# The border before the mixing: weights of group 32 in the forward stage, special columns with the others, the last spectrum store in two parts

## The chip, the cores and the metric

The kernel runs on one core of one Trainium2 chip. The metric is the device time of one execution in microseconds (us), as the median of several runs. Beside it there is one execution that the hardware profiler recorded; all durations of single instructions are taken from that one.

## The reference

The input x is `(16, 16, 256, 256)` in float32: 16 images, 16 channels, 256 rows, 256 columns. Two layers are computed, each of the form x + f(group norm of x).

```python
# layer 0: 3x3 circular convolution, written in the frequency domain
Kx = jnp.fft.ifft2(x, norm='ortho')
z = jnp.einsum('oihw,bihw->bohw', Lw, Kx)
y = jnp.real(jnp.fft.fft2(z, norm='ortho'))
...
# layer 1: Laplace operator with poles and residues
alpha = jnp.fft.fft2(x, axes=(-2, -1))
A = 1.0 / (omega1[:, None, None, None] - weights_pole1[None])
Bm = 1.0 / (omega2[:, None, None, None] - weights_pole2[None])
S = jnp.einsum('ikpq,oikp,xikq->oxik', weights_residue, A, Bm)
output_residue1 = jnp.einsum('biox,oxik->bkox', alpha, S)
output_residue2 = jnp.einsum('bikpq,ikpq->bkpq', D, weights_residue)
x1 = jnp.fft.ifft2(output_residue1, axes=(-2, -1)).real
x2 = jnp.einsum('kbiqz,biqx->kizx', F, E2).real
return x1 + x2 / Nx / Ny
```

S mixes the 16 input channels into 16 output channels with a matrix of its own for every frequency. That product is the mixing stage below; the two-dimensional transform before it is the forward stage.

## The kernel before

There are four stages after one another, which share one SBUF and one set of queues.

1. The convolution with its norm (`conv`, up to line 713), some 565 us. Its result v goes to DRAM in `vD`.
2. The forward transform (lines 716 to 980), until about 1197 us. Its loop goes over 64 units: channel i, outer, and four images at a time. In each unit `fold` makes even and odd parts, `lines` transforms one direction on TensorE, and `columns` the other; the first result is copied to SBUF as `q` (L833) and combined on VectorE into the spectrum tile `spec` (L837 to L840). `first_slots` sets a few special columns (L848 on VectorE, L849 on GpSimd), and after the four units of a channel `project` multiplies (`pr`, L865, VectorE) and adds (`proj`, L866, GpSimd), and `spec` is stored to `aD` in DRAM (L976). The spectrum tile alternates between two pools, `spec_even` and `spec_odd`; the last channel uses `spec_odd`. The last store goes through ScalarE's queue, the others through SP's.
3. The mixing (lines 984 to 1248), until about 1860 us: 32 groups of frequencies. A row of `aD` for a partition is one frequency of the other direction; group g takes partitions 4g to 4g+3. For each group a tile of mixing matrices `sg` is made: `weights(g)` computes small pole terms on VectorE (L903 to L919) and spreads them into `w` (L930 on GpSimd; for group 0 four copies on ScalarE, L927); `sums` multiplies `w` with the constant table `ct` on TensorE (L1032), and `spread` puts the result into `sg`, one half by ScalarE (L1049), one by a shuffle on VectorE (L1052). `mix` is the product with the loaded spectrum `abd` (L1120), its result goes through `yt` (L1233) to `yD` in DRAM (L1134). While group g is mixed in four quarters n, the sums of group g+1 are made, one quarter ahead of each mixing.
4. The inverse transform (lines 1251 to 1451).

The border that matters here is `first_sums` (L1054): the matrices of group 0. That group holds two special frequencies, so the halves of its `sg` come from two sets of weights, those of group 0 and those of an extra group 32. `first_sums` clears `abd01` (L1058), computes the weights of 0 (begun in the forward stage) and of 32, loads the first spectrum quarters (`load`, L1102), adds `accs` (L1062), goes through two halves h of four quarters n with sums and spreads, and fixes one column of each half with a copy of the other set's column, kept in `other` (L1078, L1079). Between the quarters it computes the weights of group 1. At the end it clears `abd2` and `abd3` (L1081) and loads them (L1107). `finish_projections` then forms `o2` from `accs` and the constant `jmat` (L1090 to L1092), and the loop over groups begins.

Three things set the order. Instructions run on each engine's queue in the order in which the program emits them, except that the framework moves what is emitted outside the stages with a written order (`manual_schedule`) to where its inputs are free. Pools of different stages lie over each other in SBUF: a tile of the mixing may be written when the tile of the forward stage that lay there has been released by its last reader, a store included. `abd3` and the second `sg` pool (`sg1`) lie over `spec_odd`. And a DMA's issue waits in SP's queue behind the one before it[...].

Of the kernel before, what the change touches and what calls it, by code (L numbers as in the profile page):

```python
# [16 lines left out]
B = 16  # L17
# [7 lines left out]
def conv_then_laplace_kernel(ctx: ExitStack, tc: tile.TileContext, a: dict, out: bass.AP):  # L25
# [36 lines left out]
    o2 = cp.tile([P, B, 2, 16], FP, name="o2", tag="o2")  # L62
    proj = cp.tile([P, 2, B, 16, 2], FP, name="proj", tag="proj")
    jmat = cp.tile([P, 3, P], FP, name="jmat", tag="jmat")
# [93 lines left out]
    nc.sync.dma_start(out=jmat, in_=a["jmat"])  # L158
# [573 lines left out]
    u0 = pool(p1, "u0")  # L732
# [140 lines left out]
    up = {"v": pool(p2, "v", side="right"), "u0": u0}  # L873
# [21 lines left out]
    def weights(g):  # L895
# [4 lines left out]
        u = up["u" if g else "u0"].tile([P, 4, 32, 4], FP, name="u", tag="u")  # L900
# [19 lines left out]
        if g == 0:  # L920
            yield
# [3 lines left out]
        if g == 0:  # L925
            for i in range(4):
                nc.scalar.activation(w4[:, :, i], v2, AF.Copy, scale=m4[:, i : i + 1])  # L927
            return wt
# [14 lines left out]
    last, first_weights = None, weights(0)  # L943
    for u in range(len(units) + 1):
# [23 lines left out]
        if u == len(units) - 4:  # L968
            first_constants()
        if len(units) - 4 < u < len(units):  # L970
            next(first_weights)
        if last is not None:
            first_slots(b0, spec, *done)
            if b0 == B - 4:
                project(i, psd)
                (nc.sync if i + 1 < C else nc.scalar).dma_start(  # L976
                    out=aD[:, 2 * i : 2 * i + 2], in_=spec.rearrange("p r f b -> p r (f b)")
# [20 lines left out]
    def new_sg(g):  # L998
        return (g0, g1)[g % 2].tile([P, N, 2 * C], FP, name="sg", tag="sg")
# [8 lines left out]
    zp.tile([P, 384], FP, name="between", tag="between")  # L1008
# [16 lines left out]
    def sums(n, w):  # L1025

        ps = [pg.tile([P, 2, N], FP, name="ps_s", tag="ps_s") for _ in range(2)]
        for q in range(2):
            for iq in range(4):
                for odd in range(2):  # L1030
                    rows = slice(64 * odd, 64 * odd + 64)
                    nc.tensor.matmul(  # L1032
                        ps[odd][32 * iq : 32 * iq + 32, q],
                        lhsT=w[rows, iq, 2 * n + q],
                        rhs=ct[rows, iq, 2 * n + q],
# [18 lines left out]
    def first_sums():  # L1054
# [4 lines left out]
        wt, w128 = at_once(first_weights), at_once(weights(32))  # L1059
        load(0, 1)  # L1060
        steps, w1 = weights(1), None
        nc.vector.tensor_tensor(accs, proj[:, :, :, :, 0], proj[:, :, :, :, 1], ALU.add)  # L1062
        sg = new_sg(0)
        other = up["u"].tile([P, 2, 2 * C], FP, name="other", tag="other")
        for h, w in enumerate((wt, w128)):
            for n in range(4):
                fy = slice(P * h, P * h + P)
                ps = sums(n, w)
                spread(
                    n,  # L1070
                    (sg[:, fy], [z[:, :, fy].rearrange("p q n -> p n q") for z in ps]),
                    (other[:, 1 - h], [z[:, :, P * (1 - h)] for z in ps]),
                )
                if 4 * h + n in (3, 4, 5):
                    w1 = next_step(steps, w1)
# [534 lines left out]
```

## Time and profile before

| | |
|---|---|
| median of 3 runs | 2617.32 us |
| lowest and highest | 2607.34 and 2626.05 us |
| the profiled execution's own time | 2623.94 us |
| its span, first to last instruction | 2622.1 us |
| mean granted TensorE clock | 0.986 |
| TensorE (PE) busy | 2468.6 us |
| VectorE (DVE) busy | 1980.8 us |
| moved by DMA | 653.17 MB |

The page of the profile gives busy times by engine, then the span in 40 slices of 65.6 us, then the DMA queues, then the chain of work that ended last, and then the costliest groups of instructions. The timeline shows single instructions by their start; an idle time in brackets names what ended it. ACTq and SPq rows are DMA issues in the queues of ScalarE and SP. "PEld" is TensorE's load of weights, which runs beside its matmuls.

### The profile page before, as it was taken

To read this page: it belongs to the slowest core of one execution; us is meant where nothing else is said; L and a number is where in the kernel's file an instruction comes from. 1 tells how busy PE (TensorE), PEld (TensorE's weight loads), DVE (VectorE), ACT (ScalarE), POOL (GpSimd) and SP (SyncE) were. 2 spreads that over 40 slices of the span, in tenths; PEclk is the share of its full clock that TensorE was granted. 3 is DMA by queue.
4 is the path that set the end of the run, shared out by engine and by line. 5 is a ranking of instruction groups with operands and counts; after the bars stand their busy time and mean duration, and the time that the engine had idled before them with its cause. 6 is when DMAs were issued, how large, how long until landed. Compare 5 with 4: busy or idle time off the path is not lost.

```text
span 2622.1 us, 84262 instructions
## 1 busy us (share of the span) xinstructions
PE 2468.6 (94%) x35314; PEld 1885.3 (72%) x35314; DVE 1980.8 (76%) x3772; ACT 1432.6 (55%) x2599; POOL 1290.5 (49%) x1179
## 2 busy tenths in 40 slices
PE   5998999989999999998999999999799999999998
PEld 2444455567777777775878778788688888888887
DVE  7777788848888888887877878887276676667666
ACT  2565566666666666665666656666244444444443
POOL 1333378433333333333666645766555565555553
PEclk9999999989999999999999999999899999999999
DMA  7888878854655655655777777777988888888884
GB/s 274 276 279 282 294 270 294 297 211 177 240 195 209 242 220 194 245 225 190 225 229 214 226 225 222 222 227 228 253 302 289 291 292 279 299 289 287 291 287 174
DMA packets 318011, 653.17 MB, mean 249 GB/s; under 512 B 49174, under 2 KB 163990, under 8 KB 305728
## 3 DMA queue, kind: packets, MB, share of 16 engines
q1 hardware_dynamic: 316464, 640.57, 72.4%
q8 instruction: 278, 4.55, 0.7%
q0 software_dynamic: 896, 3.02, 0.4%
q10 hardware_dynamic: 272, 4.19, 0.4%
q14 instruction: 101, 0.83, 0.1%
HBM read 368.15 MB, written 280.36 MB: 247 GB/s over the span
## 4 chain that ended last, share of the span: by engine, by line
PE 58%; DVE 7%; DMA 4%; SPq 3%; ACT 3%; POOL 2%; issue 1%; ACTq 0%; DVEq 0%; POOLq 0%
PE ps_mix L1120 9%; PE ps_y L777 9%; PE ps_y L785 8%; PE ps_p L1361 7%; PE ps_f L1385 7%; PE ps_f L1386 7%; PE ps_x L820 5%; DMA yD<-yt 4%; PE ps_s L1032 2%; SPq L1134 2%; PE ps_h L1345 2%; PE psd L805 1%; DVE r L1394 1%; DVE ol L1396 1%; DVE ol L1397 1%
## 5 line engine op out<-in xcount | busy, mean ns | idle before, releaser
L1120 PE MATMUL ps_mix<-abd,sg 128*64 128x128 f32 x8192 | 482.2, 276 | 39.4 <-DMA yD<-yt 16.6
L1120 PEld LDWEIGHTS ps_mix<-abd,sg 128*64 128x64 f32 x8192 | 451.9, 138 | 92.9 <-ACT yt L1233 55.7
L1325 POOL TENSOR_TENSOR u<-yk 128x512 f32<-128x512 f32 (+1 forms) x268 | 358.2, 1369 | 314.7 <-PE ps_p L1361 249.1
L305 PE MATMUL ps_conv<-xt,wc 32*32 32x512 f32 x12288 | 445.6, 602 | 36.0 <-issue 26.1
L305 PEld LDWEIGHTS ps_conv<-xt,wc 32*32 32x32 f32 x12288 | 251.1, 103 | 217.6 <-issue 127.0
L793 ACT ACTIVATE t<-ps_y,vmr 128x384 f32<-128x384 f32 x512 | 297.1, 580 | 161.1 <-PE ps_y L785 161.1
L1052 DVE STREAM_SHUFFLE sg<-ps_s 128x512 f32<-128x512 f32 (+1 forms) x264 | 329.1, 1316 | 0.0
L777 PE MATMUL ps_y<-tabE,vq 128*128 128x256 f32 x1024 | 313.2, 388 | 11.0 <-DVE vq L766 9.4
L785 PE MATMUL ps_y<-tabO,vq 128*128 128x256 f32 x1024 | 305.9, 380 | 0.0
L275 POOL TENSOR_TENSOR pair<-pair,far 128x1024 f32<-128x1024 f32 x64 | 151.7, 2370 | 304.1 <-DVE pair L272 207.7
L1385 PE MATMUL ps_f<-pt,inv 128*128 128x256 f32 x1008 | 300.4, 380 | 0.0
L1386 PE MATMUL ps_f<-hs,ey 128*128 128x256 f32 x1008 | 299.8, 379 | 0.0
L1361 PEld LDWEIGHTS ps_p<-inv,u 128*128 128x128 f32 x2048 | 268.9, 193 | 35.4 <-POOL u L1329 10.9
L1389 DVE TENSOR_TENSOR r<-ps_f,q 128x256 f32<-128x256 f32 x256 | 107.0, 418 | 241.9 <-ACT q L1388 241.9
L1361 PE MATMUL ps_p<-inv,u 128*128 128x128 f32 x2048 | 276.2, 278 | 9.8 <-POOL u L1329 9.7
L1049 ACT ACTIVATE sg<-ps_s,mcol 128x512 f32<-128x512 f32 (+1 forms) x264 | 179.3, 689 | 192.2 <-DVE sg L1052 117.1
L777 PEld LDWEIGHTS ps_y<-tabE,vq 128*128 128x128 f32 x1024 | 189.6, 191 | 87.5 <-ACT q L833 51.2
L1388 ACT COPY q<-ps_f 128x256 f32<-128x256 f32 x256 | 95.4, 373 | 274.7 <-PE ps_f L1386 250.4
L1363 ACT COPY pt<-ps_p 128x512 f32<-128x512 f32 x256 | 151.5, 592 | 134.9 <-PE ps_p L1361 134.9
L765 POOL TENSOR_TENSOR vq<-vf 128x512 f32<-128x512 f32 x64 | 81.4, 1272 | 291.6 <-DVE vf L769 281.5
L785 PEld LDWEIGHTS ps_y<-tabO,vq 128*128 128x128 f32 x1024 | 195.4, 191 | 26.9
L1233 ACT COPY yt<-ps_mix 128x512 f32<-128x512 f32 x352 | 184.1, 592 | 55.8 <-DMA yD<-yt 42.2
(237 smaller groups left out, 3993.6 us busy)
## 6 DMA issues: line engine op xcount, KB each, us to landing
xt<-in_x SPq DMA_DIRECT2D x288, 258.0 KB
vD<-pair SPq DMA_DIRECT2D x256, 256.0 KB
yD<-yt SPq DMA_DIRECT2D x512, 128.0 KB
vl<-vD SPq DMA_DIRECT2D x128, 512.0 KB
out_y<-ol SPq DMA_DIRECT2D x128, 512.0 KB
s<-vD SPq DMA_DIRECT2D x126, 512.0 KB
aD<-spec SPq DMA_DIRECT2D x15, 4096.0 KB
yk<-yD SPq DMA_DIRECT2D x60, 1024.0 KB
```

What stands on the lines that cost most here:

```text
L305: nc.tensor.matmul(acc[r][32 * c : 32 * c + 32], lhsT=ready[b][0][rows, phase, tap], rhs=halves[b][u // 2][rows, q : q + 5 : 4, 2 - tap : ...
L777: nc.tensor.matmul(ps[:, 0:N], lhsT=vf[:, xo, 0, j], rhs=tabE[:, 0 : i + 2 : i + 1], start=True, stop=False, skip_group_check=True,)
L785: nc.tensor.matmul(ps[:, P : P + N], lhsT=vf[:, xo, 1, j], rhs=tabO[:, i : C + 1 : C - i], start=False, stop=True, skip_group_check=True,)
L793: nc.scalar.activation(t[:, xo, j].rearrange("p l n -> p (l n)"), ps[:, 0:384], AF.Copy, scale=vmr[:, 0, b0 + j, i : i + 1],)
L1049: nc.scalar.activation(to[..., k : k + 2], src[odd], AF.Copy, scale=nsgn)
L1052: nc.vector.stream_shuffle(to[..., C + k : C + k + 2], src[1 - odd], swap)
L1120: nc.tensor.matmul(ps[64 * t : 64 * t + 64, j], lhsT=sg[:, f : f + 2].rearrange("p f m -> p (f m)"), rhs=abd[jq][:, :, 2 * t + cc, 2 * jj ...
L1233: (nc.vector.tensor_copy if m >= (2 if late else 3) else nc.scalar.copy)(o, src)
L1325: nc.gpsimd.tensor_tensor(u[:, :, j].rearrange("p b (c n) -> p c b n", c=8), in0, in1, o)
L1361: nc.tensor.matmul(ps[:, at], lhsT=u[:, n], rhs=tab, start=True, stop=True)
L1385: nc.tensor.matmul(ps[:, e], lhsT=tab, rhs=pt[:, e], start=True, stop=False)
L1386: nc.tensor.matmul(ps[:, e], lhsT=ey[:, e], rhs=hs, start=False, stop=True)
```

## The change

- The weights of group 32 are computed in the forward stage, as those of group 0: the steps of both are spread over the last six units (before: those of group 0 over the last three), and both are spread into `w` by ScalarE.
- In `sums` the weights of group 32 are multiplied with the halves of `ct` in turned order, so that the 128 columns that are needed and the first column of the other half lie side by side. `sg` of group 0 has one column more (257), each spread takes 129 columns, and `other` is copied from `sg` by one ScalarE copy for each half.
- The weights of group 1 are computed in the loop, ahead of the first mixing; group 0 then makes no sums in its first quarter, one set in the second and in the third, and two in the fourth.
- The last spectrum store is cut: partitions 0 to 15, all that the first four groups read, go first through ScalarE's queue; partitions 16 to 127 go through SP's queue, behind the issue of the first load.
- `accs` is added on GpSimd. `jmat` is loaded at the border into the memory of `s_ex`, and `o2` takes the memory of `proj`; the room under "between" becomes 320 columns, and `u0` and `v` get two buffers.

```diff
-    o2 = cp.tile([P, B, 2, 16], FP, name="o2", tag="o2")
-    jmat = cp.tile([P, 3, P], FP, name="jmat", tag="jmat")
...
-    nc.sync.dma_start(out=jmat, in_=a["jmat"])
...
-    u0 = pool(p1, "u0")
+    u0 = pool(p1, "u0", 2)
...
-    up = {"v": pool(p2, "v", side="right"), "u0": u0}
+    up = {"v": pool(p2, "v", 2, side="right"), "u0": u0}
...
-        u = up["u" if g else "u0"].tile([P, 4, 32, 4], FP, name="u", tag="u")
+        u = up["u" if g % 32 else "u0"].tile([P, 4, 32, 4], FP, name="u", tag="u")
...
-        if g == 0:
+        if g % 32 == 0:
...
-    last, first_weights = None, weights(0)
+    last, first_weights = None, [weights(0), weights(32)]
...
-        if u == len(units) - 4:
+        if u == len(units) - 7:
             first_constants()
-        if len(units) - 4 < u < len(units):
-            next(first_weights)
+        if len(units) - 7 < u < len(units):
+            next(first_weights[(u - len(units)) // 3 + 2])
         if last is not None:
             first_slots(b0, spec, *done)
             if b0 == B - 4:
                 project(i, psd)
+                rows = slice(0, P if i + 1 < C else 16)
                 (nc.sync if i + 1 < C else nc.scalar).dma_start(
-                    out=aD[:, 2 * i : 2 * i + 2], in_=spec.rearrange("p r f b -> p r (f b)")
+                    out=aD[rows, 2 * i : 2 * i + 2],
+                    in_=spec[rows].rearrange("p r f b -> p r (f b)"),
                 )
...
-        return (g0, g1)[g % 2].tile([P, N, 2 * C], FP, name="sg", tag="sg")
+        return (g0, g1)[g % 2].tile([P, N + 1 - g % 2, 2 * C], FP, name="sg", tag="sg")[:, 0 : N + (g == 0)]
...
-    zp.tile([P, 384], FP, name="between", tag="between")
+    zp.tile([P, 320], FP, name="between", tag="between")
...
-    def sums(n, w):
+    def sums(n, w, turned=False):
...
+                    c = ct[rows, iq, 2 * n + q].rearrange("p (h n) -> p h n", h=2)
                     nc.tensor.matmul(
-                        ps[odd][32 * iq : 32 * iq + 32, q],
+                        ps[odd][32 * iq : 32 * iq + 32, q].rearrange("p (h n) -> p h n", h=2),
                         lhsT=w[rows, iq, 2 * n + q],
-                        rhs=ct[rows, iq, 2 * n + q],
+                        rhs=c[:, ::-1] if turned else c,
...
-        wt, w128 = at_once(first_weights), at_once(weights(32))
+        wt, w128 = (at_once(steps) for steps in first_weights)
         load(0, 1)
-        steps, w1 = weights(1), None
-        nc.vector.tensor_tensor(accs, proj[:, :, :, :, 0], proj[:, :, :, :, 1], ALU.add)
+        nc.sync.dma_start(
+            out=aD[16:P, 2 * C - 2 : 2 * C], in_=spec[16:P].rearrange("p r f b -> p r (f b)")
+        )
+        nc.gpsimd.tensor_tensor(accs, proj[:, :, :, :, 0], proj[:, :, :, :, 1], ALU.add)
...
-                fy = slice(P * h, P * h + P)
-                ps = sums(n, w)
+                ps = sums(n, w, h == 1)
+                fy = slice(P * h, P * h + P + 1)
                 spread(
-                    n,
-                    (sg[:, fy], [z[:, :, fy].rearrange("p q n -> p n q") for z in ps]),
-                    (other[:, 1 - h], [z[:, :, P * (1 - h)] for z in ps]),
+                    n, (sg[:, fy], [z[:, :, 0 : P + 1].rearrange("p q n -> p n q") for z in ps])
                 )
-                if 4 * h + n in (3, 4, 5):
-                    w1 = next_step(steps, w1)
+            nc.scalar.copy(other[:, 1 - h], sg[:, P * (1 + h)])
...
+    jmat = ep.tile([P, 3, P], FP, name="jmat", tag="s_ex")
+    nc.sync.dma_start(out=jmat, in_=a["jmat"])
...
+        o2 = cp.tile([P, B, 2, 16], FP, name="o2", tag="proj")
...
-    ahead, wt = first_sums()
-    finish_projections()
+    ahead, wt = first_sums(), None
+    o2 = finish_projections()
...
-            evict = sums(n, w_now) if ahead is not None else []
+            if g == 0 and n == 0:
+                w_now = at_once(weights(1))
+            sets = () if ahead is None else (n,) if g else ((), (0,), (1,), (2, 3))[n]
+            evict = [(j, sums(j, w_now)) for j in sets]
             yt = yp.tile([P, 2, 4 * B, 16], FP, name="yt", tag="yt")
-            if evict:
-                spread(n, (ahead, [z.rearrange("p q n -> p n q") for z in evict]))
+            for j, ps in evict:
+                spread(j, (ahead, [z.rearrange("p q n -> p n q") for z in ps]))
```

More of the change, by code (lines that the diff above doesn't have):

```diff
@@ L924, in weights @@
         w4 = wt.rearrange("p a k (i m) -> p (a k) i m", i=4)
-        if g == 0:
+        if g % 32 == 0:
             for i in range(4):
@@ L1082, in first_sums @@
             load(0, jq)
-        return sg, w1
+        return sg
+    jmat = ep.tile([P, 3, P], FP, name="jmat", tag="s_ex")
+    nc.sync.dma_start(out=jmat, in_=a["jmat"])
     def finish_projections():
+        o2 = cp.tile([P, B, 2, 16], FP, name="o2", tag="proj")
         for ro in range(2):
@@ L1092, in finish_projections @@
             nc.vector.tensor_copy(o2[:, :, ro], ps)
+        return o2
     def load(g, jq, rows=range(4)):
```

## The prediction

> **What bounds the kernel now.** I read the page from the top: busy times, slices, then the chain.
>
> ```profile
> span 2622.1 us, 84262 instructions
> PE 2468.6 (94%) x35314; PEld 1885.3 (72%) x35314; DVE 1980.8 (76%) x3772; ACT 1432.6 (55%) x2599; POOL 1290.5 (49%) x1179
> PE   5998999989999999998999999999799999999998
> PE 58%; DVE 7%; DMA 4%; SPq 3%; ACT 3%; POOL 2%; issue 1%; ACTq 0%; DVEq 0%; POOLq 0%
> ```
>
> TensorE (PE) is busy nearly everywhere and leads the chain. The whole edit acts in one gap: the border between the forward stage and the mixing, near 1200 us. So the timeline of the window 1180 to 1260 us is the view that decides. Columns: start, length, engine, line, what, and in brackets the idle time before with its releaser.
>
> ```profile
> 1190.19 6.93 POOL L1058 MEMSET abd<- 128x8192 f32 x1 [0.31 <-POOL spec L849]
> 1190.99 1.69 ACT L927 ACTIVATE w<-v,mcol 128x256 f32<-128x256 f32 x4
> 1196.91 1.28 DVE L865 TENSOR_TENSOR pr<-psd,coef 128x512 f32<-128x512 f32 x2
> 1197.46 0.39 ACTq L976 DMA_DIRECT2D aD<-spec  x1
> 1198.11 0.98 DVE L903 TENSOR_TENSOR u<-kgrp,pims 128x128 f32<-128x128 f32 x1
> ...
> 1203.03 0.72 DVE L1052 STREAM_SHUFFLE sg<-ps_s 128x256 f32<-128x256 f32 x1
> ...
> 1204.59 6.72 PE L1032 MATMUL ps_s<-ct,w 64*32 64x256 f32 x128 [9.01 <-ACT other L1049]
> ...
> 1209.20 2.57 SPq L1102 DMA_DIRECT2D abd<-aD  x4
> ...
> 1215.35 1.89 POOL L930 TENSOR_TENSOR w<-v,mcol 128x1024 f32<-128x1024 f32 x1 [10.50 <-DVE v L919]
> ...
> 1217.18 6.97 POOL L1081 MEMSET abd<- 128x4096 f32 x2
> ...
> 1219.12 4.00 PE L1120 MATMUL ps_mix<-abd,sg 128*64 128x128 f32 x64
> ```
>
> VectorE (DVE) leads: weights of group 32 from 1198.11 to 1202.4, `accs` until 1203.0, then 32 shuffles with the weights of group 1 between them, until the first mixing starts at 1219.12. Then TensorE goes at a beat of 4.67 us per quarter group (1.02 of sums, 3.65 of mixing, in the chain), with the second, third and fourth mixing at 1224.07, 1228.74 and 1233.41, and the first of group 1 at 1239.19. That last start is my yardstick: the mixing behind it is TensorE at its beat, so a shift there reaches the end.
>
> The table by stretches shows the last store and the clock (columns: us, busy of PE, PEld, DVE, ACT, POOL with counts, clock, DMA share, GB/s):
>
> ```profile
> 1196.00:1198.00 2.00, 0.00 (x0) 0.00 (x0) 2.00 (x7) 0.00 (x0) 1.76 (x4) 1.00 0.00 0
> 1204.00:1206.00 2.00, 1.41 (x32) 0.68 (x32) 2.00 (x11) 1.68 (x6) 0.85 (x1) 0.50 1.00 426
> 1208.00:1210.00 2.00, 1.88 (x40) 1.11 (x32) 1.84 (x11) 1.47 (x6) 0.00 (x0) 0.50 0.03 8
> ```
>
> The 4.19 MB store moves data from 1198 to 1208 (the DMA view of 1195 to 1240 gives its queue 22.0% of 45 us, 9.9 us), and TensorE, idle from 1195.6 to 1204.6, comes back at clock 0.50 until about 1210.
>
> [...]
>
> **The change, part by part.**
>
> (a) Weights of 32. Eight DVE instructions leave the border: 1198.11 to 1202.42, 4.3 us. In the forward stage they add about 2.7 us of DVE work (0.28+0.29+0.29+0.94+0.25+0.34+0.28+0.28) over six units of 9.6 us, in which TensorE sets the pace and DVE waits 1.96 to 4.71 us per unit for ScalarE (ACT): nothing, and without that cover 2.7 us. The product moves from POOL (2.21 us) to four more ACT instructions. The built order puts six of the eight copies ahead of the first q copy and two ahead of the second. Six at 0.42 from 1190.99 end at 1193.55; before, the q copy began at 1192.95. The chain q, spec, pr is 0.6 us later: +0.6, and pr ends at 1198.8.
>
> (b) accs to POOL: -0.6 us of DVE; on POOL some 1.4 us (nearest row: 1.37 for 128x512) behind proj, done near 1202.3, needed only by `ps_o`.
>
> (c) Special columns. 16 DVE shuffles of 2 elements go (each pushes the next by about 0.17), 16 of ACT too; two ACT copies and a wait each way come, some 0.4 us each: -2.0 us. [...]
>
> (d) Weights of 1 leave the shuffles: DVE ran them at 1209.7 to 1215.1 in the border for 3.1 us. They now run after the first mixing's inputs, while that mixing runs. -3.1 us.
>
> (e) So shuffles start at 1198.8. A quarter costs about 1.25 us warm (2 x 0.55 of DVE, plus a TensorE round of 1.02 through four PSUM buffers), 1.95 at half clock as at 1204.6 to 1206.6. Eight quarters, some cold: 10 to 12 us, plus 1.2 for the fix. First mixing at 1210.4 to 1212, 7 to 9 us before 1219.12. It has no sums of group 1 in front of it. It ends near 1215.
>
> (f) The store in two. Small: issued at 1198.05. Around its data the old store took 1.84 us (1197.46 to 1209.20 less 9.9). Data: 1.24 us if the rate holds (9.9/8)[...]. I take 3.0 as middle: landed at 1202.9 (1201.1 to 1204.9). SP then issues the four loads (2.57), and the large store at 1205.5. The loads took until about 1215.0 after an issue at 1209.2, 5.8 us, so they land at 1208.7, in time for (e). Behind them the large store: 9.9 x 112/128 = 8.7, to 1217.4, plus 1.2 of receipt as before: 1218.6. jmat waits for the last line transform only and is in SBUF near 1193: nothing.
>
> (g) What is late next. abd3 lies in the memory of the last spectrum tile. In before its memset waits for the one store, over by 1209, and the product w of group 1 (POOL L930) runs ahead of both memsets. In the built order of the changed kernel the memset of abd3 waits for both stores, and the product for group 1 stands behind it on POOL. TensorE's queue has the sums with those weights between the first and the second mixing. So: large store 1218.6, memset 3.52, product 1.89, sums at 1224.2. TensorE, idle from 1215, comes back cold: mixing costs 475 instead of 273 ns there, so 43% of about 4.7 us, 2.0 us. Second mixing ends at 1224.2+1.02+3.65+2.0 = 1230.9; third +4.67 = 1235.6; fourth with two sums +2.04+3.65 = 1241.3; sums 1.02: first mixing of group 1 at 1242.3. Before: 1239.19.
>
> (h) Three small loads of SP move from 497.6 to the first 50 us, jmat leaves there: both in queues TensorE does not wait for; 0, and 1 us either way without that.
>
> Sum at the yardstick: -4.3-0.6-2.0-3.1+0.6 = -9.4 at the first mixing (-7 to -9 by timeline with the cold rounds), then all of it lost at the new wait: +3.1. On the profiled execution's 2623.94 us (span 2622.1) that is 2627.0; that execution is 6.6 us over the median of the runs, 2617.32, so for the median 2620.4.
>
> **Rivals.**
> B, the wait does not bind. Were the product ahead of the abd3 memset in effect, or the store done by 1210, group 1's weights would be there and the border keep its 7 to 9 us: 2609.5. For it: only DMA times stand between. Against: the store would need to move 3.67 MB in under 2 us. A partial form is likelier: small store at full rate and a warm clock give 1224.2-1.8-2.0, a yardstick of 1238.5, -0.7: 2616.6.
> C, slower: [...] +7.1, 2624.4. [...] Against: the stretch 1228 to 1230, with yD stores of 32 partitions each in it, carries 268 GB/s.
> D, much slower: the 112-partition store runs on few engines. One engine of 16 moves 4.19 MB/16 in 9.9 us; on four engines 3.67 MB take 35 us, 26 more: from there on the change is slower by over 1%, 2647; on one 139 us, 2750. [...]
> That the change does not do what it says: the built order shows every part in place.
>
> **How the numbers follow.** A (the wait takes the gain, +1 to +5) 0.53; C 0.17; B in its partial form 0.15, full 0.08; D 0.03; something outside the border 0.04, half each way. I predict A, 2620.4. Its own range, with the bounds of the small store and the clock, is 2618 to 2623. Single runs of before spread by 19 us, a median moves by some 8, so the range is 2604 to 2636. A change of 1% is 26 us, about what a measurement of this kernel tells from none; the border itself is 25 us long. Faster 0.02, same 0.93, slower 0.05 (D and half of the unknown).
>
> **What would show it.** First mixing at 1210 to 1212; the x128 sums with a shorter wait; then TensorE idle some 9 us before the second round of sums, released by POOL's product w; a memset of abd3 alone near 1218 with a DMA named ahead of it; clock 0.50 after it; first mixing of group 1 at 1240 to 1244. Wrong if the second mixing starts before 1222 (B), if the large store lands after 1225 (C, D), or if anything moves before 1150 us.

## The result, and the profile after

| | before | after |
|---|---|---|
| median (22 runs of each, side by side) | 2616.90 us | 2623.64 us |
| lowest and highest | 2607.34 and 2628.43 us | 2617.13 and 2629.23 us |
| profiled execution's own time | 2623.94 us | 2625.39 us |

The ratio is 1.0022, with a 95% interval of 1.0011 to 1.0032: 5.8 us slower, between 2.9 and 8.4 (the means lie 5.7 us apart, the medians 6.7). That is within 1%, and nearly twice the 3.1 us forecast.

The page of the kernel after, with the lines that answer to those of before:

```profile
span 2622.5 us, 84218 instructions
PE 2465.7 (94%) x35314; PEld 1889.0 (72%) x35314; DVE 1986.0 (76%) x3739; ACT 1433.8 (55%) x2589; POOL 1288.7 (49%) x1179
PE 58%; DVE 7%; DMA 5%; SPq 4%; ACT 2%; issue 2%; POOL 1%; DVEq 0%; ACTq 0%; POOLq 0%
```

It is hardly different: VectorE and ScalarE issue 33 and 10 instructions fewer, and in the chain DMA and SP's queue have a point more each. The two spans differ by 0.4 us only, because the two executions differ before the border: TensorE started the forward stage at 574.7 us before and at 568.2 after (what that is, the run with the early loads alone looks into). So all times at the border are counted here from the start of the last projections on TensorE (the last row of `psd`, x14), at 1191.15 us in the execution before and at 1184.61 after, and written with a plus. In the timeline of the kernel before, that mark and the yardstick of the prediction, the first mixing of group 1, are these lines:

```profile
1191.15 0.66 PE L805 MATMUL psd<-t,hB 128*32 128x128 f32 x14 [0.34 <-ACT t L793]
...
1239.19 3.71 PE L1120 MATMUL ps_mix<-abd,sg 128*64 128x128 f32 x64 [1.04 <-DMA yD<-yt]
```

The timeline of the kernel after around the border:

```profile
1184.61 0.66 PE L802 MATMUL psd<-t,hB 128*32 128x128 f32 x14 [0.33 <-ACT t L790]
...
1190.95 0.34 ACTq L974 DMA_DIRECT2D aD<-spec  x1
...
1197.60 2.57 SPq L1106 DMA_DIRECT2D abd<-aD  x4
...
1200.27 0.53 SPq L1061 DMA_DIRECT2D aD<-spec  x1
...
1205.37 3.81 PE L1124 MATMUL ps_mix<-abd,sg 128*64 128x128 f32 x64 [0.81 <-DVE sg L1078]
...
1215.12 3.51 POOL L1080 MEMSET abd<- 128x4096 f32 x1 [16.51 <-DMA aD<-spec]
...
1218.60 1.89 POOL L927 TENSOR_TENSOR w<-v,mcol 128x1024 f32<-128x1024 f32 x1
...
1220.55 1.96 PE L1032 MATMUL ps_s<-ct,w 64*32 64x256 f32 x32 [11.38 <-POOL w L927]
...
1222.44 4.22 PE L1124 MATMUL ps_mix<-abd,sg 128*64 128x128 f32 x64
...
1237.81 3.71 PE L1124 MATMUL ps_mix<-abd,sg 128*64 128x128 f32 x64
```

Read it upwards from the sums of group 1 at 1220.55. TensorE idles 11.38 us ahead of them, and the releaser is GpSimd's product `w`. That product starts the moment a memset ends, and the memset, of `abd3`, had GpSimd idle for 16.51 us until a DMA of `spec` was over: the large part of the store, issued at 1200.27. The first mixing, in between, starts at 1205.37. In the clock of the border:

| | before | forecast | after |
|---|---|---|---|
| first loads issued | +18.05 | +11.75 | +12.99 |
| first mixing | +27.97 | +19.25 to +20.85 | +20.76 |
| large store issued | | +14.35 | +15.66 |
| large store over (memset of `abd3` starts) | | +27.45 | +30.51 |
| sums ahead of the second mixing | +31.90 | +33.05 | +35.94 |
| first mixing of group 1 | +48.04 | +51.15 | +53.20 |

The change gains 7.2 us up to the first mixing and is 5.2 us behind at the first mixing of group 1.

The stretches of the kernel after (the last three columns are TensorE's clock, the busy share of the DMA engines, and GB/s):

```profile
1190.00:1192.00 2.00, 0.00 (x0) 0.00 (x0) 2.00 (x6) 0.00 (x0) 1.34 (x4) 1.00 0.82 90
...
1194.00:1196.00 2.00, 2.00 (x48) 1.50 (x40) 1.17 (x5) 0.84 (x2) 1.92 (x3) 0.50 1.22 131
...
1206.00:1208.00 2.00, 2.00 (x41) 2.00 (x38) 1.90 (x7) 1.12 (x2) 0.00 (x0) 1.00 1.01 401
...
1220.00:1222.00 2.00, 1.45 (x32) 0.67 (x32) 0.00 (x0) 0.00 (x0) 0.49 (x1) 0.50 0.65 195
```

In the first two the small store is on its way. For a full share of the engines it moves 110 and 107 GB/s, a quarter of what the whole store of before moved (393 GB/s at a share of 0.93, which makes 423):

```profile
1206.00:1208.00 2.00, 2.00 (x48) 0.84 (x32) 1.33 (x9) 1.04 (x4) 0.00 (x0) 0.50 0.93 393
```

The view counts a packet whole in the stretch in which it starts, so that a share can pass 1 (1.22 here), and the stretch between those two reads low (0.39). The sum over the whole small store does not depend on that. It is the line of its queue in the DMA view of the kernel after, 1190 to 1216 us (packets, MB, share of the 16 engines' time):

```profile
q10 hardware_dynamic: 48, 0.52, 18.7%
```

18.7% of 26 us are 4.9 us of all 16 engines, where the whole store of before, eight times as much data, took 9.9. In the stretch of 1206, the large store is on its way. In the last, TensorE is back from its idle time at clock 0.50.

### The profile page after: what moved, and what is told of

Read it like the earlier page. It is cut to its first block, busy times and chain, and to the rows that moved or that the text cites. A ratio compares the mean times of both kernels' runs of the same rounds, so it can differ in the third digit from the quotient of the medians.

```text
span 2622.5 us, 84218 instructions
## 1 busy us (share of the span) xinstructions
PE 2465.7 (94%) x35314; PEld 1889.0 (72%) x35314; DVE 1986.0 (76%) x3739; ACT 1433.8 (55%) x2589; POOL 1288.7 (49%) x1179
## 4 chain that ended last, share of the span: by engine, by line
PE 58%; DVE 7%; DMA 5%; SPq 4%; ACT 2%; issue 2%; POOL 1%; DVEq 0%; ACTq 0%; POOLq 0%
PE ps_mix L1124 10%; PE ps_y L774 9%; PE ps_y L782 8%; PE ps_p L1368 7%; PE ps_f L1392 7%; PE ps_f L1393 7%; PE ps_x L817 5%; DMA yD<-yt 4%; PE ps_s L1032 2%; SPq L1138 2%; PE ps_h L1352 2%; DVE ol L1404 2%; PE psd L802 1%; DVE r L1401 1%; DVE ol L1403 1%
## 5 line engine op out<-in xcount | busy, mean ns | idle before, releaser
L302 PEld LDWEIGHTS ps_conv<-xt,wc 32*32 32x32 f32 x12288 | 256.9, 103 | 203.2 <-issue 115.0
L1368 PEld LDWEIGHTS ps_p<-inv,u 128*128 128x128 f32 x2048 | 268.0, 193 | 36.2 <-POOL u L1336 11.7
```

Source lines behind the costliest of these rows:

```text
L302: nc.tensor.matmul(acc[r][32 * c : 32 * c + 32], lhsT=ready[b][0][rows, phase, tap], rhs=halves[b][u // 2][rows, q : q + 5 : 4, 2 - tap : ...
L1368: nc.tensor.matmul(ps[:, at], lhsT=u[:, n], rhs=tab, start=True, stop=True)
```

## The experiments

Each ratio below is against runs of the kernel before on the same chip; the groups of runs were on different chips (medians of before from 2615.18 to 2617.92 us), so ratios are compared, not times. "First of group 1" is the first mixing of group 1, the yardstick of the prediction.

| run | first mixing | first of group 1 | time against before (95%) |
|---|---|---|---|
| before | +27.97 | +48.04 | 1 |
| after | +20.76 | +53.20 | 1.0022 (1.0011 to 1.0032) |
| e1_product_first | +20.49 | +49.34 | 1.0003 (0.9989 to 1.0016) |
| e2_one_store | +26.36 | +47.90 | 0.9996 (0.9980 to 1.0012) |
| e3_split_only | +28.06 | +47.46 | 1.0008 (0.9997 to 1.0019) |
| e4_rows_32 | +20.52 | +53.87 | 1.0027 (1.0017 to 1.0036) |
| e6_large_at_once | +28.36 | +49.75 | 1.0014 (1.0004 to 1.0025) |
| e7_large_at_once_product_first | +28.38 | +50.44 | 1.0004 (0.9988 to 1.0020) |
| e8_early_loads_only | +29.38 | +48.05 | 0.9993 (0.9981 to 1.0006) |
| e9_split_and_weights_32 | +26.14 | +48.56 | 1.0004 (0.9992 to 1.0017) |
| h1_abd3_elsewhere | +20.53 | +43.96 | 1.0002 (0.9987 to 1.0017) |
| h2_abd3_elsewhere_sums_later | +20.54 | +43.73 | 0.9991 (0.9974 to 1.0007) |
| h2_again (the same kernel) | +20.59 | +43.66 | 0.9997 (0.9983 to 1.0011) |
| h3_large_behind_all_loads | +20.55 | +47.74 | 0.9998 (0.9984 to 1.0012) |

In time, only after, e4 and e6 stand apart from before, all three by being slower. So the causes are read at the yardstick, from one profiled execution of each version.

My theory after the result: the mechanism of the forecast is right (the product behind the memset of `abd3`, the memset behind the large store). The rivals: the large store's traffic itself is what costs, whatever waits for it; or the loss comes from another part of the change.

### The product ahead of the memset

```diff
         for jq in range(2, 4):
+            if jq == 3:
+                w1 = at_once(weights(1))
             nc.gpsimd.memset(abd[jq], 0.0)
             load(0, jq)
-        return sg
+        return sg, w1
...
-            if g == 0 and n == 0:
-                w_now = at_once(weights(1))
```

> Clocked from the start of the last projections (TensorE, psd x14), the first mixing of group 1 stood at +48.0 us before and at +53.2 after. Only the order on POOL changes: the product w of group 1 stands between the two memsets instead of behind both. Theory (the gain was lost because this product, and with it TensorE's sums, stood behind a memset that waits for the large store): TensorE's 11.4 us wait ahead of the second mixing is gone, the second mixing starts near +26 (after: +37.8). What still waits for the large store (+30.5) is the memset of abd3 and the writing of the sums of group 1, so the fourth mixing starts at +38 to +40 and the first of group 1 at +43 to +45: 8 to 10 us under after, 3 to 5 under before, a time near 2614. Rival (the order is not what decides; the large store holds the writing of the sums and abd3 just as long): the stall moves to the third and fourth mixing, the first mixing of group 1 stays at +50 or later, and the time is that of after within 2 us.

TensorE's wait was gone: the sums came at +25.59 behind an idle time of 0.92 us, and the second mixing at +26.62, 11 us earlier than in after. Yet the first mixing of group 1 came at +49.34, not at +43 to +45: of 11 us, 4 were left. The timeline of this run shows what had stepped into the gap:

```profile
1202.49 21.61 SPq L1113 DMA_DIRECT2D abd<-aD  x8
...
1217.11 3.51 POOL L1082 MEMSET abd<- 128x4096 f32 x1 [5.45 <-DMA aD<-spec]
...
1219.72 5.38 PE L1126 MATMUL ps_mix<-abd,sg 128*64 128x128 f32 x64 [2.24 <-ACT yt L1240]
...
1224.21 2.02 SPq L1140 DMA_DIRECT2D yD<-yt  x4
...
1228.15 1.56 ACT L1240 COPY yt<-ps_mix 128x512 f32<-128x512 f32 x3 [4.73 <-DMA yD<-yt]
```

SP spent 21.61 us on the eight loads of `abd2` and `abd3`: those of `abd3` wait for the same memset. The four y stores of the first quarter stand behind them in SP's queue and were issued at 1224.21, so ScalarE, with the first quarter's `yt` buffer still in use, waited 4.73 us to evict the third mixing. The third mixing itself had waited for evictions that stood behind the writing of `sg1`, which lies over the same spectrum tile. So the theory was right on TensorE's wait and wrong on what that wait alone is worth: three more things waited for the large store, the clearing and loading of `abd3`, the y stores behind those loads, and the writing of `sg1`.

### One store

```diff
-                rows = slice(0, P if i + 1 < C else 16)
...
-                    out=aD[rows, 2 * i : 2 * i + 2],
-                    in_=spec[rows].rearrange("p r f b -> p r (f b)"),
+                    out=aD[:, 2 * i : 2 * i + 2], in_=spec.rearrange("p r f b -> p r (f b)")
...
-        nc.sync.dma_start(
-            out=aD[16:P, 2 * C - 2 : 2 * C], in_=spec[16:P].rearrange("p r f b -> p r (f b)")
-        )
```

> The last spectrum tile is stored in one piece again (ACT's queue), all else as in after. Theory (the split costs more than it gives): loads start at +18 and land at +24, so the first mixing starts at +24 (after: +20.8); but the memset of abd3 starts at +18, the product is there at +23.5, and TensorE never idles behind the first mixing: second mixing +29, first of group 1 +43.5 to +45, 8 to 10 us under after and 3 to 5 under before; time near 2614. Rival (the split earns its 3 us at the first mixing, and the loss of after comes from other parts of the change): the first mixing of group 1 at +53 or later, time 2623 or more.

```profile
1205.60 2.57 SPq L1101 DMA_DIRECT2D abd<-aD  x4
```

```profile
1212.22 5.71 PE L1119 MATMUL ps_mix<-abd,sg 128*64 128x128 f32 x64 [5.09 <-DMA abd<-aD]
...
1233.76 3.71 PE L1119 MATMUL ps_mix<-abd,sg 128*64 128x128 f32 x64
```

(The first is the timeline of SP, the second of TensorE; the last projections start at 1185.86.) Without the split the kernel is 5.3 us ahead of after at the yardstick, though its first mixing is 5.6 us later: nothing waits once it has begun. The forecast of a gain over before failed (+47.90 against +48.04). The store took 13.4 us from its issue to the first load (11.7 before), and the loads 6.6 us from their issue until the mixing, so the mixing started at +26.4 and not at +24, and with TensorE back from 5.09 us of idling: the granted clock was 0.50 from 1210 to 1214 us, and the mixing took 5.71 us where a later one takes 3.71. With one store, VectorE's shorter path ends in front of a wait for the loads, which began at +21.3. The rival, that the split is worth its 3 us, is excluded at the yardstick, where it costs; in time the intervals of the two still touch (0.9980 to 1.0012 here, 1.0011 to 1.0032 in after).

### The split alone, on the kernel before

```diff
+                rows = slice(0, P if i + 1 < C else 16)
...
+                    out=aD[rows, 2 * i : 2 * i + 2],
+                    in_=spec[rows].rearrange("p r f b -> p r (f b)"),
...
         load(0, 1)
+        nc.sync.dma_start(
+            out=aD[16:P, 2 * C - 2 : 2 * C], in_=spec[16:P].rearrange("p r f b -> p r (f b)")
+        )
         steps, w1 = weights(1), None
```

> Only the split, on the kernel before: 16 partitions of the last spectrum tile first, the other 112 behind the four first loads. Theory: VectorE binds here (weights of 32, shuffles, special columns, weights of 1), so the first mixing stays at +28 (within 0.5), the product stands ahead of both memsets, and abd3 is loaded by +39, before the fourth mixing at +42: first mixing of group 1 at +48 (within 1), time that of before within 2 us. Rival (the large store itself disturbs what runs beside it): +50 to +53, a time 3 us or more over before.

First mixing at +28.06, first of group 1 at +47.46, as expected; the time is 2.1 us over before, at the edge of what was expected, with an interval that holds 1. The first mixing comes so late that the large store is nearly over when its memory is needed. One wait for it is left, though the profile names another releaser: TensorE had the sums of group 1 ready at about 1216.6, and ScalarE wrote the first of them into `sg1` at 1218.18, which is +29.74 and 0.6 us after the store's last packet (+29.11).

```profile
1218.18 0.71 ACT L1051 ACTIVATE sg<-ps_s,mcol 128x512 f32<-128x512 f32 x1 [2.47 <-POOL abd L1086]
```

That wait did not reach the yardstick. The same large store that costs 5 us at the yardstick behind a short path costs nothing there behind a long one, so its traffic alone is not the cause.

### Twice the partitions in the small store

```diff
-                rows = slice(0, P if i + 1 < C else 16)
+                rows = slice(0, P if i + 1 < C else 32)
...
-            out=aD[16:P, 2 * C - 2 : 2 * C], in_=spec[16:P].rearrange("p r f b -> p r (f b)")
+            out=aD[32:P, 2 * C - 2 : 2 * C], in_=spec[32:P].rearrange("p r f b -> p r (f b)")
```

> As after, with 32 partitions instead of 16 in the first part of the last store (1.05 MB), 96 in the second. In after the first part took 6.65 us from issue to the first load, 1.84 of it fixed, so 4.8 us for 0.52 MB, 109 GB/s. If the partitions reached limit it [...], twice as many partitions move twice the bytes in the same time: 6.5 to 7 us again. If the number of engines or a fixed rate limits it: 11 to 12 us. If it was only the start of the transfer: under 6. First mixing of group 1 at +51 to +54 in the first case, and the time that of after within 3 us; 5 us more in the second.

Issued at 1190.85, first load at 1197.71: 6.86 us, against 6.65 with half the bytes. The stretches of this run:

```profile
1190.00:1192.00 2.00, 0.00 (x0) 0.00 (x0) 1.97 (x6) 0.00 (x0) 1.34 (x4) 1.00 0.62 131
...
1194.00:1196.00 2.00, 2.00 (x48) 1.06 (x40) 1.50 (x6) 0.98 (x2) 1.98 (x2) 0.50 1.27 262
```

For a full share of the engines that is 211 and 206 GB/s, where 16 partitions gave 110 and 107, and all 128 gave 423. The store's queue took 19.5% of 26 us of all 16 engines, 5.1 us, against 4.9 for half the bytes. So the rate rose with the partitions that the store reaches, 16, 32 and 128 of them, and its bytes rose with them (0.52, 1.05 and 4.19 MB); no run here takes the two apart or shows what behind them sets the rate. The first mixing of group 1 and the time came as expected in this case.

### The large store at once

```diff
+                if i + 1 == C:
+                    nc.scalar.dma_start(
+                        out=aD[16:P, 2 * i : 2 * i + 2],
+                        in_=spec[16:P].rearrange("p r f b -> p r (f b)"),
+                    )
...
-        nc.sync.dma_start(
-            out=aD[16:P, 2 * C - 2 : 2 * C], in_=spec[16:P].rearrange("p r f b -> p r (f b)")
-        )
```

> As after, but the large part of the last store is issued on ACT's queue right behind the small one, at about +7 from the start of the last projections, not behind the first loads at +15.7. Theory (the border of after is set by when the large store is over, since the memset of abd3, behind it the product w of group 1 and on SP the y stores wait for it): the large store is over at about +18, the memset of abd3 at +21.7, the product at +23.6, while the first mixing still runs (+20.8 to +24.6). TensorE's wait of 11.4 us is gone: second mixing at +25 to +27, first of group 1 at +40 to +43 (after +53.2, before +48.0), a time 10 to 13 us under after, near 2611. Rival (the loads, issued at +13 beside it, have to share the DMA engines with the large store and land behind it): first mixing at +24 to +26, first of group 1 at +45 to +48, a time of 2615 to 2617.

The rival's mechanism held, and the times came out later than its ranges. Stretches and timelines of this run (SP's, then TensorE's):

```profile
1198.00:1200.00 2.00, 0.00 (x0) 0.00 (x0) 1.87 (x7) 0.14 (x1) 1.33 (x4) 1.00 1.21 131
1200.00:1202.00 2.00, 0.80 (x16) 0.68 (x24) 2.00 (x7) 1.24 (x4) 1.92 (x3) 0.63 0.42 41
1202.00:1204.00 2.00, 2.00 (x48) 1.46 (x40) 1.18 (x5) 0.93 (x2) 2.00 (x2) 0.52 0.91 90
```

```profile
1205.95 7.17 SPq L1108 DMA_DIRECT2D abd<-aD  x4
```

```profile
1220.66 5.56 PE L1126 MATMUL ps_mix<-abd,sg 128*64 128x128 f32 x64 [6.41 <-DMA abd<-aD]
```

From 1198 to 1204, 0.52 MB were moved, at 41 to 131 GB/s: that is the small store alone, so the large one, next in the same queue, got nothing until it was through. Then the large store was in the loads' way: their issue took 7.17 us where it had taken 2.57, and the first mixing waited for them until +28.36. The memset of `abd3` started at +25.1; with the large store over at +18, the theory would have had it there.

With the product moved between the memsets as well (the diff of the run with the product ahead, on top):

> The same, and the product w of group 1 between the two memsets on POOL. Theory: with the large store over at +18 nothing waits for the product's place, so this is within 1 us of the run with the large store at once, at every mixing and in time (within 2 us). Rival (the memset of abd3 starts later than +20, so that the product still comes late behind it in that run): 2 to 6 us less than there at the second mixing.

First of group 1 at +50.44, 0.7 us later than without: the order on GpSimd no longer mattered, as expected, though for the reason that the first mixing was late, not that the store was early. Its issue of the four loads took 7.26 us. Its time is not told apart from that of the run without, nor from before.

### The early loads alone, on the kernel before

Only `jmat` and `o2` as the change has them; the loads of the three small tables p2k, kgrp and mcol then move as in after.

```diff
-    o2 = cp.tile([P, B, 2, 16], FP, name="o2", tag="o2")
-    jmat = cp.tile([P, 3, P], FP, name="jmat", tag="jmat")
...
-    nc.sync.dma_start(out=jmat, in_=a["jmat"])
...
+    jmat = ep.tile([P, 3, P], FP, name="jmat", tag="s_ex")
+    nc.sync.dma_start(out=jmat, in_=a["jmat"])
...
+        o2 = cp.tile([P, B, 2, 16], FP, name="o2", tag="proj")
...
```

> The kernel before with only this part of the change: jmat loaded at the border and o2 in the memory of proj, with which the three small loads of SP (p2k, kgrp, mcol) move from about 497 us into the first 50. In the profiles so far TensorE started the forward stage at 574.7 and 572.0 us with the late loads and at 567.7 to 568.7 us in four with the early ones. Theory one (SP's issue is on the path near 500 us, and its three loads, some 3 us with their issue, delay what follows): the forward stage starts at 568 to 569, the border stays as before (+48), and the time is 3 to 5 us under before, 2612 to 2614. Theory two (executions differ by that much in the first stage anyhow): time that of before within 2 us.

Theory two is the better one: 0.9993, an interval that holds 1, the border at +48.05. With the early loads the forward stage started at 569.0 us here and at 567.7 to 569.1 in eight others, but at 575.9, 573.6 and 575.5 in those of e6, h1 and h3, which have them too. So executions differ by 8 us there, and after's 6.5 us are within that; a gain of up to 5 us from the loads isn't excluded. The first mixing came 1.4 us later than in before, though the border differs in `jmat` and `o2` only: one round of sums ahead of it took 2.16 us instead of 1.22. Two traces of nearly the same border can differ by that much there.

### The split and the weights of group 32, on the kernel before

The early loads, the split, and the weights of 32 in the forward stage on the kernel before; special columns, `accs` and the weights of group 1 stay as they were. To the diffs of two runs above (e3, e8) come these lines, and with them the second buffers of `u0` and `v` and the two conditions on `g % 32` as the change has them:

```diff
-    last, first_weights = None, weights(0)
+    last, first_weights = None, [weights(0), weights(32)]
...
-        if u == len(units) - 4:
+        if u == len(units) - 7:
...
-            next(first_weights)
+            next(first_weights[(u - len(units)) // 3 + 2])
...
-        wt, w128 = at_once(first_weights), at_once(weights(32))
+        wt, w128 = (at_once(steps) for steps in first_weights)
```

> The kernel before with the early loads, the split of the last store and the weights of group 32 in the forward stage; special columns and weights of group 1 as before. With the split alone the first mixing was at +28.1 and the first of group 1 at +47.5. Theory (eight VectorE instructions, 4.3 us, leave the path, and the ACT copies in front of the first q cost 0.4 to 0.6): first shuffle 3.7 to 3.9 us earlier, first mixing at +24.2 to +24.6; the product stands ahead of both memsets, abd3 is loaded by +36 to +37, ahead of the fourth mixing at +38.8: first of group 1 at +43.5 to +45, a time near 2614. Rival (the shuffles start earlier, but wait for the sums or the first loads): first mixing at +26 or later, first of group 1 at +46 or later.

The theory was wrong on the gain. First shuffle at +10.07 where the split alone had +11.88: 1.8 us, not 3.7 to 3.9. VectorE's and ScalarE's timelines of this run show both waits:

```profile
1194.28 0.69 DVE L1064 TENSOR_TENSOR accs<-proj 128x512 f32<-128x512 f32 x1 [2.00 <-POOL proj L863]
```

```profile
1215.16 0.70 ACT L1048 ACTIVATE sg<-ps_s,mcol 128x512 f32<-128x512 f32 x1 [5.19 <-DMA aD<-spec]
```

`accs` stands on VectorE in front of the first shuffle and waits 2.00 us for GpSimd's `proj`; before, the weights of 32 had filled that time. And as soon as the first mixing is 1.9 us earlier, ScalarE waits for the large store with the writing of `sg1` (5.19 us), so the first mixing of group 1 is at +48.56.

### abd3 in other memory

```diff
-    kp.tile([P, 1024], FP, name="between", tag="between")
+    kp.tile([P, 256], FP, name="between", tag="between")
...
     tp = pool(p2, "ct")
-    a2 = pool(p2, "abd3")
     g1 = pool(p2, "sg1")
+    zq = pool(p2, "gap")
+    a2 = pool(p2, "abd3")
...
+    zq.tile([P, 400], FP, name="gap", tag="gap")
```

> As after, but abd3 lies behind sg1, in memory that the last spectrum tile does not use (3 KB less padding between the two spectrum tiles makes the room), so its memset has no store to wait for; only the writing of the sums of group 1 (sg1 lies over that tile) still does. POOL's order, the split and SP's order stay. Theory (in after the memset behind the large store held the product w of group 1, TensorE's sums, the loads of abd3 and, behind them on SP, the y stores): memset of abd3 at about +14, product at +25.6, second mixing at +26 to +27, third at +33 to +34 (ScalarE and VectorE still wait with the sums of group 1 until the large store is over at +30.5), and no wait for y stores: first mixing of group 1 at +44.5 to +46.5 (after +53.2; with the product first +49.3; before +48.0), a time 2 to 3 us under before. Rival (what holds is the large store's traffic, or the writing of the sums alone): first of group 1 at +48 or later, a time not under that of before.

This takes away only what made the memset wait; store, split and both orders stay as in after. GpSimd's and TensorE's timelines (projections at 1190.90):

```profile
1201.40 6.96 POOL L1082 MEMSET abd<- 128x4096 f32 x2
1215.25 1.89 POOL L927 TENSOR_TENSOR w<-v,mcol 128x1024 f32<-128x1024 f32 x1 [6.88 <-DVE v L916]
```

```profile
1217.20 1.10 PE L1034 MATMUL ps_s<-ct,w 64*32 64x256 f32 x32 [1.61 <-POOL w L927]
...
1224.66 3.71 PE L1126 MATMUL ps_mix<-abd,sg 128*64 128x128 f32 x64 [1.69 <-ACT yt L1242]
...
1234.86 3.71 PE L1126 MATMUL ps_mix<-abd,sg 128*64 128x128 f32 x64
```

Both memsets run as one block, the product waits for VectorE only, TensorE for 1.61 us, and the first mixing of group 1 is at +43.96: 9.2 us earlier than in after and 4.1 earlier than in before. So the overlap of `abd3` with the stored tile, with all that stood behind it, is what cost. In time the two ratios, 1.0002 and 1.0022, lie 5.2 us apart with intervals that overlap a little. The forecast gain of 2 to 3 us over before does not show: the interval of 1.0002 goes from 3.4 us gained to 4.4 lost.

With the sums of group 1 a quarter later:

```diff
-            sets = () if ahead is None else (n,) if g else ((), (0,), (1,), (2, 3))[n]
+            sets = () if ahead is None else (n,) if g else ((), (), (0, 1), (2, 3))[n]
```

> The same, and the sums of group 1 come one quarter later: none before the second mixing, two sets before the third, two before the fourth, so that their writing, which waits for the large store, stands behind the evictions of the second mixing. Theory: second mixing right behind the first at +24 to +25, third at +30 to +31, fourth at +37 to +39, first of group 1 at +42.5 to +44.5, 4 to 5 us under before. Rival (the writing of four sets in two quarters holds VectorE and ScalarE, 2.6 us a set, and takes it back): first of group 1 at +46 or later.

```profile
1207.09 6.38 PE L1126 MATMUL ps_mix<-abd,sg 128*64 128x128 f32 x106 [0.45 <-DVE sg L1080]
...
1215.28 1.52 PE L1126 MATMUL ps_mix<-abd,sg 128*64 128x128 f32 x22 [1.81 <-issue]
...
1219.02 3.71 PE L1126 MATMUL ps_mix<-abd,sg 128*64 128x128 f32 x64 [0.33 <-DMA abd<-aD]
...
1230.28 3.71 PE L1126 MATMUL ps_mix<-abd,sg 128*64 128x128 f32 x64 [0.78 <-DMA yD<-yt]
```

The second mixing follows the first without a gap (x106 in one row; ahead of its last 22 matmuls TensorE stood for 1.81 us, for which the profile names no cause), but the wait behind it moved to the loads of `abd2`, which stand behind the large store in SP's queue: third mixing at +32.47, first of group 1 at +43.73, inside what was expected and only 0.2 us from h1. Its time stood nearest to a gain, so it was run once more:

> The run with abd3 elsewhere and the sums later, once more, for its interval alone: at 0.9991 (0.9974 to 1.0007) it stands apart from after (1.0022, 1.0011 to 1.0032) but not from before. Theory (the 4.3 us at the first mixing of group 1 reach the end): ratio 0.998 to 0.9993, again +43.5 to +44 at that mixing. Rival (they are given back later): ratio 0.9995 to 1.001.

+43.66 again, and 0.9997. By these ratios the two runs are 2.4 and 0.8 us under before, and neither interval leaves out 1. The second ratio falls in the range of the rival, by which the gain is given back later, and not in that of the theory; the interval holds both.

With the large store behind all first loads as well:

```diff
-        nc.sync.dma_start(
-            out=aD[16:P, 2 * C - 2 : 2 * C], in_=spec[16:P].rearrange("p r f b -> p r (f b)")
-        )
...
             load(0, jq)
+        nc.sync.dma_start(
+            out=aD[16:P, 2 * C - 2 : 2 * C], in_=spec[16:P].rearrange("p r f b -> p r (f b)")
+        )
         return sg
```

> The same as the run with sums later, and the large store is issued behind the loads of abd2 and abd3 too, so that no load has to share the engines with it. Theory: loads of abd2 and abd3 end near +21 in issue; the large store is over at +32 to +34, some 2 to 3 us later than there, and holds the writing of the sums so much longer: first of group 1 at +45 to +47. Rival (alone, it needs 10.5 us from issue instead of 14.9, and is over no later than +31): within 1 us of that run.

SP's and ScalarE's timelines (projections at 1192.54):

```profile
1213.47 1.03 SPq L1081 DMA_DIRECT2D aD<-spec  x1
```

```profile
1228.00 0.69 ACT L1051 ACTIVATE sg<-ps_s,mcol 128x512 f32<-128x512 f32 x1 [7.50 <-DMA yD<-yt]
```

The third mixing is earlier, at +30.02, but the store was issued 5.3 us later (+20.93 against +15.66), and ScalarE started to write `sg1` only at +35.5, after an idle time of 7.50 us. The profile names a y store as the last to end before it; the large store's own last packet ended at +35.05, 14.1 us behind its issue, so the wait fits that store as well. The first of group 1 came at +47.74, 0.7 us beyond the theory's range. Behind all loads the store was not quicker, and the rival's time did not come; but alone it was not tried, for y stores ran beside it.

## Why the prediction was right, and where its sizes were off

The reading was right: the gain up to the first mixing is real, and all of it is lost behind the large store, at the new wait which the built order showed. Case A gave 2620.4, with its own range 2618 to 2623 and +1 to +5 us; 2623.64 and the +5.2 us at the yardstick are just over those ends. The wide range, 2604 to 2636, would have held B and C as well, and 2623.64 is nearer to C's 2624.4, so it is the trace and not the median that speaks for A. By its steps:

- **(a) and (b), weights of 32 and `accs`.** Forecast together -4.3 (-4.3, +0.6, -0.6), measured at the first shuffle +11.88 to +7.60, -4.3. The sum is right, the shares were not: the first q copy comes 0.44 us later; the weights of 32 alone bring 1.8 (e9 against e3), because `accs` then waits 2.00 us for `proj`; the other 2.5, not 0.6, come with moving `accs` (after against e9, which differ in more than that, but `accs` and its wait are what stands ahead of the first shuffle in e9). An instruction that costs 0.6 us in a long path was a wait in a short one. The eight durations that the prediction puts into the forward stage add up to 2.95 us, not 2.7; nothing hangs on it, since from the start of that stage on TensorE to the last projections it took 616.4 us before and after.
- **(c) and (d), special columns and weights of 1.** Forecast -5.1 by the sum, and less by the timeline with cold rounds. From the first shuffle to the first mixing it was 16.1 us and is 13.2: -2.9. No run takes the two apart.
- **(e) first mixing.** Forecast 7 to 9 us earlier, measured 7.2.
- **(f) the small store.** This is the first mis-sized term: I took 3.0 us for its data, and it took 4.8 (6.65 less the 1.84 around the data). Only the 1.24 us at the full rate came from the trace of before, which has no store of so few partitions; the 3.0 was an estimate of mine that rested on no measured case. It was issued 0.6 us earlier than forecast, which took back a part. The loads still came in time for the first mixing, but the large store stands behind them on SP and was issued 1.3 us later than forecast.
- **(f) the large store.** The second: forecast 13.1 us from issue until it is over (1205.5 to 1218.6), measured 14.85. I had put the loads ahead of it and let it run alone afterwards. The loads of `abd2`, next in SP's queue, began to move at +27.3, before its last packet was through at +30.1, which is 14.5 us after its issue; where they were issued later (e3, e9) it was through 13.5 and 12.8 us after its issue. So sharing the engines with those loads may make up 1 us or more of the 1.7; no run takes away all that ran beside the store. With that it was over 3.1 us late, and so were the memset and the product, whose lengths (3.51 and 1.89) were right.
- **(g) the new wait.** Right in place, releaser and order: TensorE idle 11.38 us (forecast "some 9"), clock 0.50, product behind the memset of `abd3`. The cold clock cost 1.4 us instead of 2.0: sums 1.89 for 1.02, the mixing 4.15 for 3.65. Sum at the yardstick: +5.2 instead of +3.1. What the forecast did not see is that more than the product stood behind this store: with the product ahead of the memset (e1), only 3.9 of the 9.2 us came back that come back without the overlap (h1).
- **(h) the small loads.** 0 within a measurement's reach (e8, 0.9993). "Wrong if anything moves before 1150 us" was a bad test: 6.5 us did move there, which lies within the scatter of executions.
- **The yardstick.** "TensorE at its beat, so a shift there reaches the end" is not borne out. In the mixing of before, TensorE idled 39 us in 29 waits ahead of mixings, 16.6 of them for y stores and 13.8 for ScalarE's evictions, and a later wait can take up an earlier shift.

Of the rivals, C named both mis-sized terms, the small store and the large one slower by some 2 us each, which no trace had shown; they were slower by 1.8 and 1.7. What slowed the large one is not shown. Measured were +5.2 at the yardstick and +5.8 in time, between A's +3.1 and C's +7.1: A and C are one mechanism with two prices. B did not happen; had the memset had no store to wait for, the yardstick would have been -4.1 and not -7 to -9 (h1), since `sg1` waits too. D did not happen: in 1206 to 1208 us of after, with the large store on its way, the engines were busy all the time (1.01) at 401 GB/s.

What stays open is why 4 us under before at the yardstick (h1, h2) show in time as something between 0.5 us over and 2.4 under. Their intervals, some 4 us each way, hold both answers. The traces do not settle it: at the first mixing of group 4, h1, h2 and its repeat are 2.5, 2.5 and 2.9 us ahead of before, but e8, level with before at the yardstick, is 3.2 us behind it there, so single executions scatter by as much. No version here is shown to beat before. Against after, the first run of h2 stands apart by its interval, h1 and the second touch it; all four measurements with `abd3` elsewhere (h1, h2 twice, h3) lie at 0.9991 to 1.0002, below the whole interval of after.

## What to carry to other kernels

A transfer that was cut into an urgent and a late part keeps its memory until the late part is over (+30.5 in after, where the loads behind the urgent part were issued at +13.0): before cutting it, list everything that is to be written into that memory, and what stands behind those writes on each queue. When a path is shortened, the instruction that was cheap in the old one (`accs`, the store, the clearing of `abd3`) may be the next wait; undoing the memory overlap was worth 9 us at the yardstick here, and moving one instruction in front of the wait only 4.

## What the runs showed that I had not expected

- A store of few partitions held all DMA engines: the one of 16 partitions took 4.9 us of all 16 engines at a quarter of the full store's rate, 107 to 110 GB/s, and the store behind it in the same queue got nothing meanwhile (e6).
- With a large store in flight, the issue of other loads was slow as well: four issues took 7.17 us (e6) and 7.26 (e7) instead of 2.57.
- Versions with the same first stage end it up to 8 us earlier or later from one profiled execution to another (567.7 to 575.9 us, same loads), so absolute times of two traces can't be compared at a border of 25 us. Times counted from a mark just ahead of it repeat better, though not always to 0.1 us: h2 twice gave +43.73 and +43.66, but all but the same border in before and e8 had its first mixing at +27.97 and +29.38.
